# A prefetch hint on all five engines for the branch around a kernel's rarely used general path

## The chip, the cores and the metric

The kernel runs on one core of a Trainium2 chip. The metric is the device time of one execution in microseconds, the median of several runs. Five engines work side by side, each with an instruction stream of its own: TensorE (PE in the profile, with its weight loads as PEld), VectorE (DVE), ScalarE (ACT), GpSimd (POOL) and SyncE (SP), which here only issues transfers.

## The reference

One block of a network over x of shape (8, 512, 256), in float32: a layer norm, windowed causal attention with 16 heads of 16 and rotary positions, and a three-layer network with weights of plus and minus one, whose output passes through silu and gates the attention.

```
xn = _layernorm(x, axis=-1)
# attention: q, k rotated; window of 250 keys, causal
mask = (delta >= 0) & (delta < CONTEXT)
scores = where(mask, einsum('bhtd,bhsd->bhts', q, k) * D ** -0.5, min)
s = (softmax(scores) @ v) @ out_proj_w.T
# network: w = where(k, 1, -1)
h = s0 * (concatenate([xn, -xn]) @ w(k0));  h = relu(h) * 2
h = s1 * (h @ w(k1));                       h = relu(h) * 2
g = _silu(s2 * (h @ w(k2)))
x = x + s * g
```

## The kernel before

The work is done sequence by sequence (`b` from 0 to 7), with tokens in tiles of 128 and features in chunks of 128. Two kinds of work are interleaved on TensorE: the network's layers (`layer`, L518: per output chunk eight 16-bit matmuls for the high part and eight 32-bit ones for the low part) and the attention's scores and values (L733, L807). ScalarE makes the high parts and exponentials, VectorE the low parts and divisions, GpSimd the masks and some products.

The order is written out by hand. Every piece of work is an entry (time, cost, function) in the list `everything`; `run` sorts it by time, calls each function, and pushes follow-ups that fall due some time later on a planned clock. Inside `tc.manual_schedule` the engines' instructions stand in the order in which these functions issue them. Times are in a planned unit in which one sequence takes `SEQ` = 42; the last sequence (b = 7) begins at 294. The numbers only order the pieces: 338.06 is the last output chunk of the second layer, 339.78 and 341.65 the third layer's last two parts, 341.6 `add_up`, and 343.52 to 346.22 the output projections (`project_o`, L916).

The kernel takes a fast path that is exact only while some quantities stay within limits. While it runs, the tiles that meet the limits are counted in `counts`. `add_up` sums these counts (L975 to L978) to one integer, `whole`. After the schedule every engine loads that integer into a register (L1025), and compares it with the number of rows: if any row failed, everything is computed again in a general, slow way.

```
    n_rows = P * 2 * B * T + B * T
    found = nc.values_load(whole[0:1, 0:1], min_val=0, max_val=n_rows)
...
    with tc.If(found < n_rows):
        for b in range(B):
```

The body of the `If` (L1072 to L1088, with `shifted` from L1027) is some thousands of instructions on each of TensorE, GpSimd, ScalarE and VectorE, and it stands in each stream between the branch and the end of the program. On the other side of the branch stand a few semaphore instructions, and then the end of the program: SP waits for all transfers and engines, and a barrier of all five follows (L1144).

The last pieces of the fast path on each engine, which the prediction follows, are: the sigmoid of the gate at L584 to L590, its earlier form at L624 to L635, the output products at L928 to L945, and the stores to `out_dram` at L932 and L946. The residual is loaded at L552.

Of the kernel before, what the change touches and what calls it, by code (L numbers as in the profile page):

```python
# [34 lines left out]
def tile_attention_times_gated_ffn(  # L35
# [44 lines left out]
    B, T, E = x.shape  # L80
# [30 lines left out]
    def load_x(b, t):  # L111
        xs[b, t] = xpool.tile([P, E], F32, tag=f"x{t}", name=f"x_{b}_{t}")
        queue = nc.scalar if b == 0 and t >= NT // 2 else nc.sync
        queue.dma_start(xs[b, t], x[b, ts(t, P), :])
# [98 lines left out]
    SEQ = 42.0  # L213
# [12 lines left out]
    def run(pieces):  # L226
        clock, count_, due = 0.0, itertools.count(), []

        def follow(at, more):
            for delay, f in more if isinstance(more, list) else ():  # L230
                heapq.heappush(due, (at + delay, next(count_), f))

        for _, cost, f in sorted(pieces, key=lambda piece: piece[0]):
            while due and due[0][0] <= clock:
                at, _, g = heapq.heappop(due)
                follow(at, g())
            more = f()
            clock += cost
            follow(clock, more)
        while due:  # L240
            at, _, g = heapq.heappop(due)
            follow(at, g())
# [109 lines left out]
    def first_parts(*tiles):  # L352
        for t in tiles:
            for f in states[0].pop(("parts", t)):
                f()
# [96 lines left out]
    def stack(b, g):  # L452
        st = states[b]
        for what in ("k0", "q0", "q1"):
            t = stacks.tile([P, T], F32R, tag=what, name=f"{what}_{b}_{g}")
            rows = st["dram", what[0], int(what[1])][32 * g : 32 * g + 32]
            nc.sync.dma_start(t.bitcast(F32), rows.rearrange("p n t -> (p n) t"))
            st[what, g] = t

    def prepare(b, plain=False):  # L460

        if b == 0 or plain:
            at = dict(stats=-40, norm=-38, x=-36, k=0, q=3, v=9.2)
            dp, dv = 1.5, 1.5
        else:

            at = dict(load=9, stats=9, down=10.5, over=12, norm=16.8, k=21.8, q=24.8, v=SEQ + 0.6)
            if b == 1:
                at.update(load=18.65, stats=15, down=18, over=18.7, norm=24.8, k=26.6, q=28.4)
            dp, dv = 1.5, 1.0  # L470
            at = {n: SEQ * (b - 1) + f for n, f in at.items()}
        out = [(at["stats"], 0, lambda: stats(b))]
        if "over" in at:
            out += [
                (at["load"], 0, lambda: load_xT(b)), (at["down"], 0, lambda: lay_down(b)),
                (at["over"], 0, lambda: lay_over(b)),
                (at["norm"], 0, lambda: norm_turned(b, 0)),
                (at["norm"] + 1.2, 0, lambda: norm_turned(b, 1)),
            ]
        for t in range(NT):  # L480
            if "over" not in at:
                out += [
                    (at["norm"] + t, 0, lambda t=t: norm(b, t)),
                    (at["x"] + t, 0.25, lambda t=t: turn_x(b, t, plain)),
                ]
            out.append((at["v"] + dv * t, 0.87, lambda t=t: project_v(b, t)))
        for what in "kq":
            for n, part in enumerate("ab"):
                if b == 0 and what == "k" and not plain:

                    out += [
                        (-34.3 if n == 0 else -32.95, 0.87, lambda p=part: project(b, "k", p, 0)),
                        (at["k"] + dp * n, 0.87, lambda p=part: project(b, "k", p, 1)),
                    ]
                else:
                    out.append((
                        at[what] + dp * n, 1.75, lambda w=what, p=part: project(b, w, p),
                    ))
        return out
# [32 lines left out]
    def outputs(b):  # L532

        n = 1 if b + 1 < B else 2
        return [(f, ts(half, T // n)) for half in range(n) for f in range(EC)]
# [67 lines left out]
    def plain_ffn(b):  # L603

        st = states[b]
        for name, src, w in (("h1p", "xp", w0["l"]), ("h2p", "h1p", w1["l"])):
            h = st[name] = hpool.tile(
                [P, NF0, T], F32, tag=name[:2] + "l", name=f"{name}_{b}"
            )
            n = w.shape[1]  # L610
            for f in range(NF0):
                ps = ps_m.tile([P, T], F32, tag="mm", name=f"f_h_{b}_{f}")
                for c in range(n):
                    nc.tensor.matmul(
                        ps, w[:, c, ts(f, P)].bitcast(F32), st[src][:, c, :],
                        start=(c == 0), stop=(c == n - 1),
                    )
                nc.scalar.activation(h[:, f], ps, AF.Relu)
# [36 lines left out]
    def finish_ffn(b, u, how):  # L655
        quick.add(last_at(b, u))
        out = [(last_at(b, u), L3 * (2 if b + 1 < B else 1), lambda: last(b, u, how))]
        if how == "later":
            out.append((late(b, u) - 4.5, 0, lambda: gate_ready(b, u)))
        return out  # L660
# [157 lines left out]
    def keep(b, g, po):  # L818

        st = states[b]  # L820
        if g % 2 == 0:
            for name, rows in (("V", first_half), ("S", second_half)):
                tile_ = st["half", name] = outs.tile(
                    [P, T], F32, tag=f"{name}{g // 2}", name=f"{name}_{b}_{g}",
                    bufs=2 if name == "V" else 1,
                )
                nc.scalar.mul(tile_, po, rows)
        else:
            for name, rows in (("V", second_half), ("S", first_half)):
                tile_ = st[name, g // 2] = st.pop(("half", name))  # L830
                nc.vector.scalar_tensor_tensor(tile_, po, rows, tile_, ALU.mult, ALU.add)
# [118 lines left out]
    def finish(b, final=False):  # L950
        out = []
        for u in range(len(outputs(b))):
            out.append((
                late(b, u), 1.75 if b + 1 < B else 0.87,
                lambda u=u: project_o(b, u, final),
            ))
        return out

    def divisions(b):
        out = []  # L960
        for pair in range(2):
            if b + 1 < B:
                first, d = (SEQ * b + 30.0, 2.0) if pair == 0 else (SEQ * (b + 1) + 4.2, 2.0)
            else:
                first, d = SEQ * b + (22.5 if pair == 0 else 33.6), 1.3
            for n in range(4):
                out.append((first + d * n, 0, lambda p=pair, n=n: invert(b, p, n)))
            out.append((first + d * 4, 0, lambda p=pair: divide(b, p)))
        return out
# [3 lines left out]
    def add_up():  # L973
# [3 lines left out]
        nc.vector.tensor_reduce(found_f, total, mybir.AxisListType.X, ALU.add)  # L977
        nc.vector.tensor_copy(whole, found_f)  # L978

    outs = None  # L980

    def swap():
# [6 lines left out]
        (-31.0, 0, lambda: enough(0)),  # L989
        (-32.7, 0, lambda: first_parts(2, 3)),  # L990
        (19.2, 0, make_w2), (22.5, 0, swap), (SEQ * (B - 1) + 47.6, 0, add_up),
    ]
    for c in range(EC):
        everything += [
# [29 lines left out]
    n_rows = P * 2 * B * T + B * T  # L1024
    found = nc.values_load(whole[0:1, 0:1], min_val=0, max_val=n_rows)  # L1025
# [43 lines left out]
                stop=(j == n // P - 1),  # L1069
            )  # L1070

    with tc.If(found < n_rows):  # L1072
        for b in range(B):
            for t in range(NT):
                load_x(b, t)
            run(prepare(b, plain=True))
            plain_ffn(b)
            for u in range(len(outputs(b))):
                run(finish_ffn(b, u, "at once"))
            for g in range(NG):  # L1080
                stack(b, g)
                po = ps_o.tile([P, T], F32, tag="po", name=f"f_po_{b}_{g}")
                for t in range(NT):
                    for r in range(4):
                        shifted(b, g, t, r, po)
                keep(b, g, po)
            run(divisions(b))
            run(finish(b))  # L1088
# [59 lines left out]
```

## Time and profile before

| | us |
|---|---|
| median of three runs | 607.96 (607.72 to 608.24) |
| profiled execution: first to last instruction (span) | 607.0 |
| what the median has around the span | 0.9 |
| TensorE busy | 594.8 (98%) |
| VectorE, ScalarE, GpSimd busy | 383.5, 294.7, 309.0 |
| last matmul ends | 598.9 |
| last compute (VectorE, L945) ends | 600.7 |

The span counts from the first to the last recorded instruction, the sequencers' own (branches, semaphores, drains) among them, while "busy" counts compute alone. In the lists, an engine's name with a q (SPq) is its sequencer. L1072 is line 1072 of the kernel.

### The profile page before, as it was taken

What the parts mean: (1) busy time and instruction counts of PE and PEld (TensorE: products, weight loads), DVE (VectorE), ACT (ScalarE), POOL (GpSimd) and SP (SyncE); (2) the same over time, 40 slices, a digit from 0 to 9 for tenths busy, and PEclk for the clock granted to TensorE, in tenths of its full rate; (3) what the DMA queues carried; (4) which work ended last, traced back from release to release, by engine and by line L of the source; (5) the groups of instructions that cost most, each with busy time, mean ns of one, the idle gap of its engine ahead of it and who ended that gap; (6) DMA issues with size and microseconds to landing.
All of it is one profiled execution on the core that took longest, in us unless ns stands there. A gap on an engine that the chain in (4) does not pass through costs nothing. (4 is left out here: it accounts for less than half of the span.)

```text
span 607.0 us, 11176 instructions
## 1 busy us (share of the span) xinstructions
PE 594.8 (98%) x4492; PEld 367.2 (60%) x4492; DVE 383.5 (63%) x606; ACT 294.7 (49%) x414; POOL 309.0 (51%) x368
## 2 busy tenths in 40 slices
PE   7999999999999999999999999999999999999994
PEld 6654666555655556556565566555666555657783
DVE  6864637558467485665856657666666557554774
ACT  4676664354554535445453454542554445555321
POOL 2975542466533663445724557235662456627632
PEclk9999999999999999999999999999999999999998
DMA  8552722226331443315243252421642216222201
GB/s 273 216 187 94 272 87 88 86 106 207 105 122 53 176 138 105 122 65 216 85 134 108 106 210 78 142 94 70 210 131 94 88 69 243 71 65 77 71 1 41
DMA packets 38061, 74.51 MB, mean 123 GB/s; under 512 B 5360, under 2 KB 13040, under 8 KB 38000
## 3 DMA queue, kind: packets, MB, share of 16 engines
q1 hardware_dynamic: 35568, 71.48, 34.0%
q10 hardware_dynamic: 2432, 2.23, 1.2%
q8 instruction: 37, 0.61, 0.4%
q14 instruction: 24, 0.20, 0.1%
HBM read 44.30 MB, written 29.39 MB: 121 GB/s over the span
## 5 line engine op out<-in xcount | busy, mean ns | idle before, releaser
L752 ACT ACTIVATE p<-sc 128x1024 f32<-128x1024 f32 (+2 forms) x144 | 138.3, 1012 | 74.9 <-PE sc L733 45.1
L768 POOL TENSOR_SCALAR_AFFINE_SELECT p<-p 128x512 f32<-128x512 f32 x128 | 91.3, 719 | 127.4 <-ACT p L752 127.4
L518 PE MATMUL h_ps<-h1l,w1l_sb 128*128 128x512 f32 (+1 forms) x576 | 146.2, 396 | 0.0
L518 PE MATMUL h_ps<-h1h,w1h_sb 128*128 128x512 f16 (+1 forms) x576 | 123.1, 356 | 0.0
L518 PEld LDWEIGHTS h_ps<-h1l,w1l_sb 128*128 128x128 f32 x576 | 100.2, 188 | 29.5 <-issue 9.2
L529 ACT ACTIVATE h2h<-h_ps 128x512 f16<-128x512 f32 (+1 forms) x72 | 39.4, 548 | 112.6 <-PE h_ps L518 112.6
L518 PEld LDWEIGHTS <-w1h_sb 128*128 128x128 f16 x576 | 51.2, 98 | 58.8 <-issue 17.5
L775 POOL TENSOR_SCALAR_AFFINE_SELECT p<-p 128x512 f32<-128x512 f32 (+1 forms) x96 | 49.3, 513 | 71.4 <-ACT p L752 71.4
L807 PE MATMUL po<-p,v_pad 128*32 128x378 f32 (+4 forms) x1216 | 76.5, 372 | 0.0
L633 DVE RECIPROCAL den<-den 128x256 f32<-128x256 f32 (+1 forms) x32 | 52.5, 1644 | 24.9 <-POOL den L628 24.9
L733 PEld LDWEIGHTS sc<-q,k 32*128 32x128 f32 x1216 | 44.2, 184 | 30.4 <-issue 21.1
L527 DVE SCALAR_TENSOR_TENSOR h2l<-h_ps,h2h 128x512 fp32r<-128x512 f32 (+1 forms) x72 | 43.8, 609 | 29.6 <-ACT h2h L529 29.6
L527 DVE SCALAR_TENSOR_TENSOR h1l<-h_ps,h1h 128x512 fp32r<-128x512 f32 x64 | 42.7, 680 | 25.7 <-ACT h1h L529 25.6
L733 PE MATMUL sc<-q,k 32*128 32x378 f32 (+4 forms) x1216 | 58.1, 306 | 0.6 <-DMA q<-dq 0.3
L884 DVE RECIPROCAL S<-S 128x128 f32<-128x128 f32 x64 | 57.5, 920 | 0.1
L518 PE MATMUL h_ps<-xl,w0l_sb 128*128 128x512 f32 x128 | 52.3, 489 | 0.0
L807 PEld LDWEIGHTS po<-p,v_pad 128*32 128x32 f32 x1216 | 31.7, 109 | 28.4 <-issue 17.0
L529 ACT ACTIVATE h1h<-h_ps 128x512 f16<-128x512 f32 x64 | 38.0, 598 | 18.7 <-PE h_ps L518 18.6
L301 DVE TENSOR_TENSOR xT<-xT,of_all 128x512 f32<-128x512 f32 x28 | 22.3, 801 | 28.4 <-DMA of_all<-d 27.9
L518 PE MATMUL h_ps<-xh,w0h_sb 128*128 128x512 f16 x128 | 38.4, 382 | 0.1
L572 PE MATMUL z_ps<-h2l,w2l_sb 128*128 128x512 f32 (+1 forms) x144 | 36.1, 391 | 0.2 <-DVE h2l L527 0.2
L425 POOL TENSOR_TENSOR m_ka<-m_ka,m_kb 128x512 f32<-128x512 f32 x16 | 20.1, 1276 | 28.5 <-DVE m_kb L404 28.5
(101 smaller groups left out, 735.1 us busy)
## 6 DMA issues: line engine op xcount, KB each, us to landing
q<-dq SPq DMA_DIRECT2D x64, 256.0 KB, 3.5
dq<-qh SPq DMA_DIRECT2D x16, 512.0 KB, 3.1
dq<-m_qa SPq DMA_DIRECT2D x16, 512.0 KB, 5.5
k<-dk SPq DMA_DIRECT2D x32, 256.0 KB, 2.7
dk<-kh SPq DMA_DIRECT2D x8, 512.0 KB, 2.9
dk<-m_ka SPq DMA_DIRECT2D x8, 512.0 KB, 2.9
x<-in_x_dram SPq DMA_DIRECT2D x30, 128.0 KB, 2.7
xT<-in_x_t_dram SPq DMA_DIRECT2D x7, 512.0 KB, 5.6
```

What stands on the lines that cost most here:

```text
L301: nc.vector.tensor_tensor(xT, xT, st["of_all"][:, i], op)
L518: nc.tensor.matmul(ph, w[p][:, c, ts(f, P)], st[src + p][:, c, cols], start=(k == 0), stop=(k == n - 1),)
L527: nc.vector.scalar_tensor_tensor(lo, ph, 0.0, hi, ALU.max, ALU.subtract)
L529: high = lambda: nc.scalar.activation(hi, ph, AF.Relu)
L572: nc.tensor.matmul(pz, w2[p][:, c, ts(f, P)], st["h2" + p][:, c, cols], start=(c == 0 and p == "h"), stop=(c == NF1 - 1 and p == "l"),)
L633: nc.vector.reciprocal(part, part)
L733: nc.tensor.matmul(sc[r // 2][:, r % 2, ds(off, n)], st["k0", g][row, ts(j, P)], st[f"q{turn}", g][row, ds(j * P + first, n)], start=(turn ...
L752: nc.scalar.activation(p[:, 2 * half : 2 * half + 2, :n], sc[half][:, :, :n], AF.Exp, scale=D ** -0.5,)
L768: nc.gpsimd.affine_select(out=block, in_=block, compare_op=ALU.is_ge, fill=0.0, base=0, pattern=[[0, 4], [1, P]], channel_multiplier=-1,)
L775: nc.gpsimd.affine_select(out=block, in_=block, compare_op=ALU.is_ge, fill=0.0, base=-1, pattern=[[0, 4], [-1, beyond]], channel_multiplier=1,
L807: nc.tensor.matmul(po[32 * r : 32 * r + 32, ds(j * P + first, n)], v_columns(j, g, r), p_[:, r, ds(off, n)], start=(j == 0), stop=(done an ...
L884: nc.vector.reciprocal(part, part)
```

## The change

One entry is added to `everything` at 338.0, which marks a place in the stream of every engine for a hint on the branch called "general"; and the `If` is given that name. Where the hint stands, each engine gets one more instruction. Nothing else in the streams is added, removed or reordered.

```diff
+    def hint():
+        tc.mark_branch_hint_location(
+            "general", "LikelyTaken", engines=list(mybir.ALL_ENGINES)
+        )
+
...
         (19.2, 0, make_w2), (22.5, 0, swap), (SEQ * (B - 1) + 47.6, 0, add_up),
+        (SEQ * (B - 1) + 44.0, 0, hint),
     ]
...
-    with tc.If(found < n_rows):
+    with tc.If(found < n_rows, label="general"):
```

## Prediction

> **What bounds the kernel now.** I read the page from the top: span, busy times, instruction queues.
>
> ```profile
> span 607.0 us, 11176 instructions
> ...
> PE 594.8 (98%) x4492; PEld 367.2 (60%) x4492; DVE 383.5 (63%) x606; ACT 294.7 (49%) x414; POOL 309.0 (51%) x368
> ...
> q8 instruction: 37, 0.61, 0.4%
> q14 instruction: 24, 0.20, 0.1%
> ```
>
> TensorE is busy for 594.8 of 607.0 us, so nearly the whole kernel is its matmuls, and the change touches none of them. What can move is the 12.2 us in which it isn't busy, most of it at the end. The two instruction queues fetch the program itself: 0.61 MB in 37 packets is 16 KB a packet, 0.20 MB in 24 is 8 KB. By the count of packets the first is TensorE's and the second the four smaller engines'.
>
> Next, the view of busy times in stretches, cut at the end of the last compute and at the end of the long gap (columns: length, then busy time and count of each engine, clock, DMA share, GB/s).
>
> ```profile
> 600.00:601.20 1.20, 0.00 (x0) 0.00 (x0) 0.71 (x2) 0.00 (x0) 0.47 (x1) 1.00 0.34 112
> 601.20:605.00 3.80, 0.00 (x0) 0.00 (x0) 0.00 (x0) 0.00 (x0) 0.00 (x0) 0.54 0.27 85
> 605.00:607.04 2.04, 0.00 (x0) 0.00 (x0) 0.00 (x0) 0.00 (x0) 0.00 (x0) 0.50 0.04 12
> ```
>
> The last compute (VectorE, L945) ends at 600.7. Then no engine does anything for over 6 us. The view of line 1072, the branch, says what the sequencers do there (engine, operation, count, ns min/median/max, first and last start).
>
> ```profile
> L1072 SPq EVENT_SEMAPHORE  x8: 17/17/17, 605.1 to 605.7; - x8
> L1072 PEldq COMPARE_BRANCH  x1: 4322/4322/4322, 598.0 to 598.0; - x1
> L1072 POOLq COMPARE_BRANCH  x1: 45/45/45, 600.1 to 600.1; - x1
> L1072 DVEq COMPARE_BRANCH  x1: 76/76/76, 601.0 to 601.0; - x1
> L1072 SPq COMPARE_BRANCH  x1: 45/45/45, 601.2 to 601.2; - x1
> L1072 ACTq COMPARE_BRANCH  x1: 54/54/54, 601.7 to 601.7; - x1
> L1072 PEldq EVENT_SEMAPHORE  x1: 51/51/51, 602.4 to 602.4; - x1
> L1072 POOLq EVENT_SEMAPHORE  x1: 17/17/17, 602.9 to 602.9; - x1
> L1072 DVEq EVENT_SEMAPHORE  x1: 21/21/21, 605.6 to 605.6; - x1
> L1072 ACTq EVENT_SEMAPHORE  x1: 17/17/17, 605.7 to 605.7; - x1
> ```
>
> From branch to next instruction: PE 4.4 us, POOL 2.8, DVE 4.6, SP 3.9, ACT 4.0. No instruction of lines 1027 to 1088 (the general path) is recorded, so every engine jumped over it, and what follows the jump is what arrives late. The waits of SP's queue put SP's gap down to nothing but itself:
>
> ```profile
> SPq L1072 <- SPq L1072: 3.8, 1, 3.8
> ```
>
> Four 8 KB packets of q14 and one of q8's lie between 601 and 604 in the DMA view cut to that stretch: fetches for these jumps. The chain that sets the end is then: last store issued (600.8), SP's branch (601.2), fetch, SP's eight semaphore instructions (from 605.1), SP's final waits and the barrier of all five (607.0). The profiled span is 607.0; the median of the runs, 607.96, has 0.9 us more around it, which I keep.
>
> [...]
>
> **The change part by part.** It adds one hint instruction to each engine's stream, and moves, if it works, five fetches from behind the branch to ahead of it.
>
> *The five hints.* The trace has no such row. Below: nothing, since the sequencers wait for their engines most of the time. [...] I take 0.05 (like the branch records) and put it at zero on the path, since something covers it on every engine. The entry sorts at 338, just before TensorE's last group of L518 matmuls (started at 589.0), behind POOL's L628 (589.1), the rectifier L529 (589.2) and VectorE's L633 (590.5); POOL then idles 2.3 us, ACT 1.4, DVE 0.4. On SP it stands before the last residual loads (L552, the last at 570.8), after which SP waits 26.2 us for the count. TensorE's sequencer runs ahead of the array: its branch executes at 598.0 while matmuls run to 598.9. [...]
>
> *The five fetches.* The same bytes, earlier. DMA is nearly idle from 583 to 590 (one packet). At zero; with no cover, a packet of 8 KB takes 0.3 to 0.5 us of one of 16 engines. From hint to branch there are 9 us or more on each engine (589 to 598 on PE, 590.5 to 601.0 on DVE, 30 on SP), twice the longest gap of 4.6.
>
> *The gap.* If SP's target is there, SP goes on at about 601.4 instead of 605.1, and likewise ACT at 601.9 and DVE at 601.2. This is up to 3.7 us. But what is late next is the stores. SP's eight instructions are one for each DMA semaphore, and they can't pass before the last store has landed:
>
> ```profile
> L946 SPq DMA_DIRECT2D out_dram<-gate x15: 337/338/347, 146.2 to 598.2; - x15
> L932 SPq DMA_DIRECT2D out_dram<-gate x2: 338/518/697, 599.9 to 600.5; - x2
> L946 ACTq DMA_DIRECT2D out_dram<-gate x1: 373/373/373, 600.8 to 600.8; - x1
> ...
> DMA to landing us min/median/max: 2.0/2.0/3.9
> ```
>
> The last stores are issued at 600.5 and 600.8. With the median landing of 2.0 us the last is in at 602.8; with the longest, 3.9 (the store of 598.2, whose landing at 602.1 fell among the fetches), at 604.7. I take 603.7, halfway: the big fetches are out of the way, but each engine, once across, will fetch a further block beside these stores, as it does now after each jump.
>
> After the landing SP needs the rest of its waits and the barrier. Now that is 607.0 − 605.1 = 1.9 us from the first of the eight; the eight take 0.6, and five of them can be done before the landing, so 1.3 to 1.7 are left; I take 1.6. The end comes at 603.7 + 1.6 = 605.3, a gain of 607.0 − 605.3 = 1.7 us. Ends: 602.8 + 1.3 = 604.1 (gain 2.9) and 604.7 + 1.7 = 606.4 (gain 0.6). The time is 607.96 − 1.7 = **606.2**, between 605.0 and 607.3.
>
> **The rivals.**
>
> *The hint does nothing (608.0).* A hint can only help if it still steers a fetch when it executes deep inside the block in which the branch lies. This is the weak place. In the stretch 563 to 601 the DMA view lists three packets on q8 and none on q14:
>
> ```profile
> q1 hardware_dynamic: 931, 0.99, 7.6%
> q8 instruction: 3, 0.05, 0.5%
> ```
>
> So the four smaller engines had their next blocks before 563, long before a hint at 589 (on SP, before 571), and TensorE fetched its last at 585.6, before 589. If the sequencer decides what to fetch only on entering a block, all five hints come too late. [...] Against: the hint has room of 9 us and a free DMA, and nothing else would be its use. Time: 607.96 + 0 to 0.1.
>
> *Only some engines profit, or the stores land late (607.0 to 607.9).* SP's final waits need all five engines across the branch. ACT branches last, at 601.7; if it alone still fetched in the shortest gap seen, 2.8 us (POOL), it would be across at 604.5, and the end at about 605.9; with its own 4.0, at 605.7 and the end where it is. PE and POOL branch early, are across at 602.4 and 602.9 now, and decide nothing.
>
> *The hint's block takes the place of one still needed (slower).* [...] If the target displaces the next block in sequence and an engine steps into that block between hint and branch, it fetches on the spot, 2.8 to 4.6 us. On VectorE that would fall on the chain L589, L590, L931, L938, L945, which issues the last store: 605.3 + 3.7 = 609.0 on the span, so about 609.9. It decides as soon as a block boundary lies among VectorE's last instructions[...]. Against it: q14 is empty from 563 to 601, so no engine crossed a boundary with a fetch there[...]. [...]
>
> **How the numbers follow.** A measurement of this kernel can tell about 0.2%, 1.2 us, from no change. The hint works on the engines that matter: 0.69, of which 0.61 gain over 1.2 us and 0.08 less (late landings, one engine left behind). It does nothing: 0.22. It displaces a needed block: 0.09. So faster 0.61, same 0.30, slower 0.09. The likeliest case gives 606.2, alone 605.0 to 607.3. To leave out no more than 2 in 10 the range must take in "nothing" with its own 0.2 us: 605.0 to 608.2; left out are the slower case and a sliver of gains above 2.9.
>
> **What would show it.** Right: a hint record on each engine near the times above; instruction packets on q8 and q14 near 570 and 588 to 592; at L1072 the next instruction within 0.3 us of the branch on SP, ACT and DVE, and a self-wait of SP there well under 3.8 us; SP's first group held by the landing of the last stores. Wrong: the same gaps of 3 to 5 us at L1072, and q14 again silent until 601 (the hint does nothing), or a new gap of about 4 us on DVE between 590 and 601 (displacement). A change in the TensorE rows before 595 would be none of this.

## The result, and the profile after

| | before | after |
|---|---|---|
| median of 21 runs each, taken side by side | 607.85 us | 606.90 us |
| ratio, after to before | | 0.9982 (0.9976 to 0.9987) |
| profiled execution: span | 607.0 us | 605.0 us |
| last compute (VectorE, L945) ends | 600.75 us | 601.15 us |
| from there to the end of the span, the **tail** | 6.29 us | 3.87 us |

By the ratio, which is taken over all runs, the change gains 0.18%, 1.1 us (0.8 to 1.5); the two medians are 0.95 us apart. The tail alone is 2.4 us shorter. So two things are to be explained: how the tail shrank, and where the other microsecond went.

The parts of the page after that answer to the first fence of the prediction:

```profile
span 605.0 us, 11181 instructions
...
PE 595.0 (98%) x4492; PEld 367.4 (61%) x4492; DVE 382.6 (63%) x606; ACT 294.6 (49%) x414; POOL 310.6 (51%) x368
...
q8 instruction: 36, 0.59, 0.4%
q14 instruction: 20, 0.16, 0.1%
```

Five instructions more, no compute more, and the busy times agree within 1.6 us. But the instruction queues carry less: q14 four packets fewer (24 to 20), q8 one fewer (37 to 36). By the numbers that is one packet for each of the five engines.

The stretches of busy time after, cut like those of before (length, busy time and count of PE, PEld, DVE, ACT, POOL, clock, DMA share, GB/s):

```profile
600.00:601.20 1.20, 0.00 (x0) 0.00 (x0) 1.12 (x3) 0.00 (x0) 0.84 (x1) 1.00 0.05 12
601.20:605.02 3.82, 0.00 (x0) 0.00 (x0) 0.00 (x0) 0.00 (x0) 0.00 (x0) 0.52 0.34 110
```

Compute ends in the first stretch, 0.4 us later than before. The empty time behind it, two stretches of 3.80 and 2.04 before, is now a single one of 3.82. Its DMA share is higher (0.34 against 0.27), since more of the stores' traffic falls into it: the stretch ahead of it has 0.05, where before it had 0.34.

The view of the branch after (line 1078 now, L1072 before; engine, operation, count, ns, first and last start):

```profile
L1078 SPq EVENT_SEMAPHORE  x8: 17/17/17, 601.8 to 603.6; - x8
L1078 PEldq COMPARE_BRANCH  x1: 393/393/393, 598.4 to 598.4; - x1
L1078 PEldq EVENT_SEMAPHORE  x1: 51/51/51, 599.4 to 599.4; - x1
...
L1078 SPq COMPARE_BRANCH  x1: 70/70/70, 601.3 to 601.3; - x1
L1078 DVEq COMPARE_BRANCH  x1: 89/89/89, 601.4 to 601.4; - x1
L1078 DVEq EVENT_SEMAPHORE  x1: 21/21/21, 602.0 to 602.0; - x1
...
```

From the branch to the next instruction it is now 0.5 us on SP, 0.6 on VectorE, 0.5 on ScalarE, 0.9 on TensorE, where it was 3.9, 4.7, 4.0 and 4.4. (GpSimd: 0.5 for 2.7.) The hint works on all five. The first row says what is late next: SP's eight instructions, packed into 0.6 us before, now stretch over 1.8. Seen one by one, five of them follow the branch at once (601.81 to 602.15), the sixth comes at 603.07 and the last two at 603.58 and 603.65. The stores explain the two late steps. The view of line 932 has SP's:

```profile
L932 SPq DMA_DIRECT2D out_dram<-gate x2: 333/336/338, 600.3 to 600.9; - x2
...
DMA to landing us min/median/max: 1.8/1.8/1.8
```

The view gives the landing of the first of the two alone. By the semaphore updates in the trace the second, issued at 600.9, lands at 603.05 and ScalarE's, the last, at 603.56; SP's sixth and seventh instruction, which wait for these two, start 0.02 us after each. In the waits of SP's queue this is still booked on SP itself, in three pieces of at most 0.9 us instead of one of 3.8:

```profile
SPq L1078 <- SPq L1078: 1.9, 3, 0.9
```

The same updates show something in the kernel before that its views don't: there SP's second store, issued at 600.5, landed only at 605.15, 4.7 us later, and in a second trace of that kernel at 605.28. Of the stores' own packets one alone moved after 603, while five fetches did (DMA view of before, cut to 603 to 607.04):

```profile
q14 instruction: 4, 0.03, 2.7%
q8 instruction: 1, 0.02, 1.5%
q1 hardware_dynamic: 1, 0.00, 0.0%
```

So two things were late at 605.1, SP's instructions behind the branch (the first at 605.1) and this store. Had all the gaps gone and this store still landed at 605.15, SP's sixth instruction would have come at about 605.17 instead of 605.53, and the tail would be some 0.4 us shorter (an estimate from these two numbers), not 2.4. With the change both come earlier. What in the fetches could hold a landing back, with the store's last packet gone at 603.0, isn't shown.

Last, the view of line 1150, the end of the schedule, where the hints are booked:

```profile
L1150 POOLq BRANCH_PREFETCH_HINT  x1: 43/43/43, 0.7 to 0.7; - x1
...
L1150 SPq BRANCH_PREFETCH_HINT  x1: 51/51/51, 0.8 to 0.8; - x1
...
```

The other three are like these, TensorE's the last: all stand at the very front of the streams, at 0.7 to 0.9 us, and not at 570 to 590. The entry at 338.0 in the plan doesn't set their place. The branches whose gaps are short now come some 600 us later, at 598.4 to 602.2 us.

The two profiles can't be compared by their spans. In the profiled executions that list both, the time is the span + 1.7 us (605.02 gives 606.75, 607.13 gives 608.86). The profiled execution of before was thus itself about 608.8 long, 0.9 above its median. The traces of before and after differ in the first 90 us only: from there on, TensorE's matmuls after stand 0.41 us behind those of before, constant to about 0.01 us, until the tail. How late the first 90 us end varies from execution to execution: two traces of one kernel, here taken three times, end them up to 0.6 us apart, and three of the kernels below were caught in executions that were 2.5 to 3.3 us behind before there. The tail can nearly be read from one trace (it repeats within 0.05 us after, and within 0.44 before). The front has to be read from medians.

### The profile page after: what moved, and what is told of

The parts are those of the page before. It is cut to its first block, busy times and chain, and to the rows that moved or that the text cites. A ratio compares the mean times of both kernels' runs of the same rounds, so it can differ in the third digit from the quotient of the medians.

```text
span 605.0 us, 11181 instructions
## 1 busy us (share of the span) xinstructions
PE 595.0 (98%) x4492; PEld 367.4 (61%) x4492; DVE 382.6 (63%) x606; ACT 294.6 (49%) x414; POOL 310.6 (51%) x368
## 5 line engine op out<-in xcount | busy, mean ns | idle before, releaser
L775 POOL TENSOR_SCALAR_AFFINE_SELECT p<-p 128x512 f32<-128x512 f32 (+1 forms) x96 | 49.3, 514 | 72.6 <-ACT p L752 69.2
L807 PE MATMUL po<-p,v_pad 128*32 128x378 f32 (+4 forms) x1216 | 76.7, 372 | 0.1
L807 PEld LDWEIGHTS po<-p,v_pad 128*32 128x32 f32 x1216 | 31.8, 109 | 28.7 <-issue 17.0
```

The costliest lines, as they stand in the source:

```text
L775: nc.gpsimd.affine_select(out=block, in_=block, compare_op=ALU.is_ge, fill=0.0, base=-1, pattern=[[0, 4], [-1, beyond]], channel_multiplier=1,
L807: nc.tensor.matmul(po[32 * r : 32 * r + 32, ds(j * P + first, n)], v_columns(j, g, r), p_[:, r, ds(off, n)], start=(j == 0), stop=(done an ...
```

## Experiments

All are timed beside the kernel before on the same chip; "time" is the ratio to it and its interval. Tail is the length defined above. "Lost" is the tail's gain (against 6.07, the mean of the two traces of before, 6.29 and 5.85) less the gain in time (the ratio times 608 us): what a kernel gives away ahead of the tail. It is good to about half a microsecond, and less so in the plain near-target kernel, which has six runs.

| kernel | hints | time | gain, us | tail, us | lost, us |
|---|---|---|---|---|---|
| before, again | none | 1.0001 (0.9990 to 1.0012) | −0.1 | 5.85 | |
| after (the result) | five, front | 0.9982 (0.9976 to 0.9987) | 1.1 | 3.87 | 1.1 |
| after, again | five, front | 0.9985 (0.9977 to 0.9993) | 0.9 | 3.84 | 1.3 |
| after, a third time | five, front | 0.9978 (0.9969 to 0.9987) | 1.3 | 3.89 | 0.8 |
| near target, plain | none | 0.9955 (0.9940 to 0.9971) | 2.7 | 3.33 | 0.0 |
| near target, hints | five, front | 0.9980 (0.9971 to 0.9989) | 1.2 | 3.30 | 1.6 |
| late | five, where planned | 0.9991 (0.9983 to 0.9998) | 0.5 | 5.50 | 0.0 |
| middle | five, inside | 0.9970 (0.9959 to 0.9981) | 1.8 | 4.16 | 0.1 |
| SP and ScalarE in front | two front, three inside | 0.9975 (0.9966 to 0.9985) | 1.5 | 3.84 | 0.7 |
| the others in front | three front, two inside | 0.9977 (0.9969 to 0.9984) | 1.4 | 3.93 | 0.7 |
| three | three, inside | 0.9972 (0.9964 to 0.9980) | 1.7 | 3.58 | 0.8 |
| three, again | three, inside | 0.9966 (0.9953 to 0.9979) | 2.1 | 3.66 | 0.3 |
| one memset more | five, inside | 0.9992 (0.9978 to 1.0006) | 0.5 | 4.20 | 1.4 |

### Both kernels again

The edit is none: the changed kernel twice more, and the kernel before once more under the same treatment.

> The changed kernel once more, for a second profile and for comparison with the others on this chip. Its profile had lost 2.4 us after the last compute (6.3 to 3.9) and was 0.4 later before it, 2.0 in all, while the timed runs lost 1.0. Theory A (the profiled execution of the kernel before overstates the gap at the branch; timed runs have a smaller one): span about 605.0 again, time about 1.0 under the kernel before. Theory B (the gap is as long in timed runs, and the hints give back over 1 us elsewhere, in the start or in the fetches): the 0.4 us ahead of the last compute is there again, and the time is again 1.0 under.

> The kernel before once more, for a second profile: its first was an execution with a tail of 6.3 us after the last compute. From the kernel with the general path left out (time 2.7 under, tail 3.3) a typical tail of 5.9 to 6.0 follows. Gaps at the branch of 2.7 to 4.7 us again; ratio 1.000 within 0.1%.

> The changed kernel on the same chip and in the same rounds as the one before. 0.9 to 1.1 under the kernel before; tail 3.9, L775 late by 0.3 again, front later by about 1 us in all.

The kernel before gives 1.0001 of itself. The changed one gives 0.9985 and 0.9978; all three intervals of it lie under 1 and overlap. So the gain is there, and about 1.1 us (for the third, 1.3 is over the 0.9 to 1.1 expected). The three tails of after agree within 0.05 us; the two of before differ by 0.44. VectorE's and SP's gaps are 4.3 and 3.4 us in the repeat, for 4.7 and 3.9: the gap varies from trace to trace, so against the repeat the tail's gain is 2.0, not 2.4. Either is well above the time gained, as theory B has it.

### A target close by, with and without hints

The body of the `If` is emptied in each stream, so that the branch jumps over a few instructions. The general path is left out of these two kernels; it isn't executed on this data. One has no hints, the other the five of the change.

```diff
+def no_general_path(nc):
+    for f in nc.m.functions:
+        for b in f.blocks:
+            if b.name.endswith("_true"):
+                b.instructions = [i for i in b.instructions
+                    if type(i).__name__ == "InstUnconditionalBranch"]
```

> No hints; the general path is left out of the program (of its block only a branch stays), so that the target of the branch is the next instruction and nothing has to be fetched out of sequence. The floor without any hint. Theory A: about 1.0 to 1.3 us under the kernel before, near the changed kernel. Theory B: 2.3 to 2.8 under the kernel before, so over 1 us better than the changed kernel. Both: in the profile the gap at the branch is under 0.5 us on each engine and the tail after the last compute about 3.6 to 3.9.

> The same as the one before without the general path, but with the five hints: what the hints alone cost, where they can gain nothing. Theory A: 0 to 0.15 us above the kernel without hints (0.1 at the start of SP's and ScalarE's first transfers). Theory B: some 1.3 us above it.

Without hints the branch of the plain kernel, in the view of line 1072:

```profile
L1072 SPq EVENT_SEMAPHORE  x8: 17/17/17, 603.6 to 605.1; - x8
...
L1072 SPq COMPARE_BRANCH  x1: 45/45/45, 603.4 to 603.4; - x1
```

SP is across in 0.2 us, the others in 0.2 to 0.3 (TensorE 0.9), and SP then waits for the stores as in the changed kernel. So the gap of before (2.7 to 4.7 us) is the price of the distance, and not of the branch, but for the 0.2 to 0.3 us that are left here, on TensorE 0.9 of 4.4 (for it the expected 0.5 was missed). This profiled execution ran late from its start (PE waited 1.8 us for the transfer of `wqkv_sb`, and its time was 608.3 where the median is 605.7), which is why 603.4 stands where after has 601.3.

This kernel also shows what the fetches do to the stores. Its DMA view from 598 to the end lists no instruction packet, and by the semaphore updates its four last stores all land 1.7 to 1.8 us after their issue, and so do those of its pair with hints. After, with five packets in that stretch, they take 1.8 to 3.2 us, and before, with ten up to the end, 2.5 to 4.7. So in these traces the last stores land later where fetches run beside them, and what the hints leave of this is most of the 0.5 us by which the tail of after (3.87) exceeds the plain one's (3.33): its last store takes 2.4 us, for 1.8 here.

The pair shows the price of the hints, because here they can gain nothing: the tails are 3.33 and 3.30. The plain kernel gains 2.7 us (1.8 to 3.6), just what its tail gives. The one with hints gains 1.2 (0.7 to 1.8). Five hints at the front cost about **1.5 us**, at five records of some 50 ns. The intervals of the two ratios only touch, so there is a cost, but with only six runs of the plain kernel its size is rough.

### The hints where the plan puts them

Each hint is moved to the place that the prediction assumed: ahead of the instruction that is last but n of its engine.

```diff
+    last_but = {"PE": 82, "DVE": 14, "Activation": 9, "Pool": 6, "SP": 10}
+    for engine, n in last_but.items():
+        own = [i for i in block.instructions if i.engine.name == engine]
+        hint, place = own[0], own[-1 - n].name
+        rest = [i for i in block.instructions if i.name != hint.name]
+        at = [i.name for i in rest].index(place)
+        block.instructions = rest[:at] + [hint] + rest[at:]
```

> The changed kernel with each hint moved from the start of its stream to the place that the plan's 338.0 stands for: before the last L518 group on PE, behind L633 on DVE, L529 on ACT, L628 on POOL, L552 on SP[...]. Theory E (what to fetch is decided when a block is entered): the gaps at the branch are back (2.8 to 4.6 us) on all five and the time is that of the kernel before, within 0.2. Theory H (a hint steers a fetch whenever it executes, 7 us or more ahead): gaps under 1 us, time that of the changed kernel or 0.1 under it.

The hints' records, in the view of line 1166 (the same place as L1150 above), and then the branch:

```profile
L1166 SPq BRANCH_PREFETCH_HINT  x1: 50/50/50, 570.4 to 570.4; - x1
L1166 PEldq BRANCH_PREFETCH_HINT  x1: 45/45/45, 587.1 to 587.1; - x1
...
L1166 DVEq BRANCH_PREFETCH_HINT  x1: 56/56/56, 590.6 to 590.6; - x1
```

```profile
L1078 SPq EVENT_SEMAPHORE  x8: 17/17/17, 604.4 to 605.0; - x8
L1078 PEldq COMPARE_BRANCH  x1: 393/393/393, 598.1 to 598.1; - x1
L1078 PEldq EVENT_SEMAPHORE  x1: 51/51/51, 599.1 to 599.1; - x1
...
L1078 SPq COMPARE_BRANCH  x1: 70/70/70, 601.3 to 601.3; - x1
...
```

The hints execute 10 to 31 us ahead of their branches. On SP, VectorE, ScalarE and GpSimd they do nothing: the gaps are 3.1, 3.65, 3.0 and 2.7 us, the whole page counts 24 packets on q14, as before, and SP's eight instructions are again packed behind a long gap. On TensorE the hint works. Its gap is 0.9 us, and the DMA view cut to 586.5 to 598 shows the fetch, where the kernel before has no packet at all:

```profile
q8 instruction: 1, 0.02, 0.5%
```

That packet, of 16 KB, moves at 589.2, two microseconds after the hint. So on TensorE the late hint started a fetch here, and on the four others, by their gaps and the 24 packets, none. Why the engines differ isn't shown; what the trace of before does show is that q14 carries no packet from 563 to 601, so that there the last fetch of the four smaller engines ahead of their branches lies before the times of all their hints here (570.4 to 590.6). Neither theory thus holds for all five. The gaps of SP, VectorE and ScalarE are shorter than in the first trace of before by 0.7 to 1.1 us, and than in its repeat by 0.2 to 0.7; TensorE's 16 KB moved at 589.2 here and at 599.89 before; whether that is what shortened them wasn't isolated. The gain of 0.5 us and the tail of 5.50 fit each other.

### The hints inside the streams

The same mover with `own[n]`, counted from the front, puts the hints behind the busy start and long before the branch. Five inside; then two halves, in which the engines named keep their hint at the front. The three lists stand below one another here; each kernel has one.

```diff
-    last_but = {"PE": 82, "DVE": 14, "Activation": 9, "Pool": 6, "SP": 10}
+    # middle:
+    first = {"PE": 1500, "DVE": 190, "Activation": 140, "Pool": 120, "SP": 90}
+    # SP and ScalarE stay in front:
+    first = {"PE": 1500, "DVE": 190, "Pool": 120}
+    # TensorE, VectorE and GpSimd stay in front:
+    first = {"Activation": 140, "SP": 90}
```

> All five hints, moved from the start of each stream to a place well inside it (behind 89 instructions on SP, 119 on POOL, 139 on ACT, 189 on DVE, 1499 on PE), so that they delay nothing in the first microseconds and still execute before the block of the branch is entered. If hints at the start cost some 1.5 us by shifting the first transfers, and a hint has to come before its block: tail after the last compute 3.8 to 3.9 as in the changed kernel, time 2.2 to 2.5 us under the kernel before (ratio about 0.996), about 1.3 under the changed kernel. If the cost comes from being armed, wherever: as the changed kernel, 1.0 under.

> SP's and ACT's hints stay at the start of their streams (ahead of all first loads), the other three are moved inside. If the cost of the start comes from the loads of the input issued 0.1 us later and in another order: tail 3.9 and time about 1.0 to 1.3 under the kernel before. If it comes from PE, DVE and POOL: about 2.3 under.

> The reverse: PE's, DVE's and POOL's hints stay at the start, SP's and ACT's are moved inside. If the loads are the cause: about 1.9 to 2.2 under the kernel before, 0.3 to 0.4 of the cost being left at L775 on POOL, which was late by that in all three kernels with a hint ahead of it and in neither of those without. If the other three engines are the cause: 1.0 under.

With five inside, at 176 to 211 us, the hints work as well as at the front (gap on SP and ScalarE 0.5, on TensorE 0.9), for branches at 598 to 602 us: to be first in its stream wasn't needed. The time is 0.9970, 1.8 us under before instead of the 2.2 to 2.5 expected; the tail of this trace, 4.16, is 0.3 longer than expected, and with it 0.1 is lost ahead of the tail. Its interval (0.9959 to 0.9981) overlaps with the change's, so that it beats the change is likely but not shown by the times. The halves give 0.9975 and 0.9977, between the two, and neither of their expected pairs of numbers is met. Which engine's hint costs how much isn't settled by the times.

The traces do isolate one part. TensorE's loads of L807 at 70 us, after, then before (an engine's wait is listed by what ended it: us, times):

```profile
L807 PEld LDWEIGHTS po<-p,v_pad x16: 106/108/110, 70.0 to 70.7; 128*32 128x32 f32 x16
...
  POOL p L768: 0.4, 1
  POOL p L775: 0.3, 1
```

```profile
L807 PEld LDWEIGHTS po<-p,v_pad x16: 106/108/109, 69.8 to 70.3; 128*32 128x32 f32 x16
...
  POOL p L768: 0.3, 1
```

A second wait of 0.3 us, for GpSimd's mask of L775, is there after and not before. The loads end 0.4 us later, and nothing downstream makes up for it: this step stays to the end of the trace. It is in every trace in which one instruction more stands ahead of L775 on GpSimd from the front (after three times, near target with hints, and the half with GpSimd in front), where TensorE falls back by 0.4 us from 65 to 75 us against before, and in none of the eight others (one memset more aside, which comes next).

### One instruction more on GpSimd, and no hint in force

To tell whether it is the hint or its place in the stream, the middle version gets one small memset among GpSimd's first instructions. At 70 us no engine has met a hint yet.

```diff
     nc.gpsimd.memset(v_pad, 1.0)
+    one_more = const.tile([P, 1], F32, name="one_more")
+    nc.gpsimd.memset(one_more, 1.0)
```

> The hints inside the streams, as in the kernel with all five moved inside, and one more instruction (a memset of 128x1) among the first on POOL, where the hint stood: every later POOL instruction moves one place up in its stream. If L775 at 69 us is late by 0.3 because of that place (the instruction then stands first in a block that has to be entered): late again here, and L807 on PE with it. If it is late because a hint is armed on POOL: on time, since the hint comes only at 190 us.

The step at L807 (L809 in this kernel) is back, 0.4 us, without a hint in force. So it is one instruction more in the stream and not the hint: a plain memset does the same. Why one place in the stream costs TensorE these 0.4 us isn't shown; that L775 then stands first in a block was the author's guess. The ratio is 0.9992 (0.9978 to 1.0006), 1.3 us above the middle version's, though the two intervals overlap; more than the step is in it. In this trace TensorE also falls back by another 0.4 us between 100 and 590 us, which happens in no other; what causes it wasn't isolated.

### Three hints are enough

TensorE and GpSimd branch early. Without their hints, and with the other three inside:

```diff
-            "general", "LikelyTaken", engines=list(mybir.ALL_ENGINES)
+            "general", "LikelyTaken",
+            engines=[mybir.EngineType.SP, mybir.EngineType.DVE, mybir.EngineType.Activation]
...
+    first = {"DVE": 190, "Activation": 140, "SP": 90}
```

> Hints on SP, ACT and DVE alone, inside the streams. PE and POOL jump early and are across by 602.9 even without, so if only the late engines matter the time is that of all five, 2.2 to 2.5 under the kernel before. If the fetches of PE and POOL (at 599.9 and 601.2) hold up the landing of the last stores, on which SP waits next: tail 4.3 to 5, time 1.2 to 2.0 under.

> The three hints on SP, ACT and DVE inside the streams, once more, beside the changed kernel on the same chip: the best version so far. Tail 3.6 to 3.9, front (time to the end of the last compute) that of the kernel before; 1.6 to 2.0 under the kernel before and 0.5 to 0.9 under the changed kernel.

From the repeat, the view of the branch:

```profile
L1078 PEldq COMPARE_BRANCH  x1: 3438/3438/3438, 598.0 to 598.0; - x1
...
L1078 PEldq EVENT_SEMAPHORE  x1: 51/51/51, 601.5 to 601.5; - x1
```

TensorE waits for 3.4 us at its branch again (4.3 before the change) and is across at 601.5; GpSimd at 602.9. The last store lands at 602.9 as well, so they hold up nothing, and the tail is 3.6 to 3.7 us, no longer than with five, where 4.3 to 5 were expected if these two fetches slowed the stores. The two runs, 0.9972 and 0.9966, are with the middle version (0.9970) the best of the kernels that keep the general path, and clearly under before. Against the change itself, in the same rounds, it is 0.9966 to 0.9978: 0.1% better by the point, with overlapping intervals, so not shown.

## Why the prediction was right, and where not

Forecast 606.2, measured 606.9, inside the range; the likeliest case (hints work, then the stores are late) is what happened. But three of its steps were wrong. Two of these cancel, by luck; the third had no effect only because the hints stood elsewhere than assumed.

**The place of the hints: wrong.** They aren't at 338 in the plan but first in each stream. In the place that the prediction worked with, the change would have gained 0.5 us, as the late version shows. Of the rivals, "the hint does nothing" named the true weak point, a hint that comes too late: in the late version, 10 to 31 us ahead of the branch, the gaps stay at 2.7 to 3.65 us on four of five engines. It was given 0.22, and with the place that was assumed it deserved more than half.

**The fetches: right in sign, not in place.** In the kernel after, one fetch per engine has disappeared by the counts (20 packets for 24 on q14, 36 for 37 on q8), q14 is empty from 563 to 601.4 as it was before, and 4 packets of it instead of 8 follow the jumps. When the target came, and in place of what, isn't shown; no trace shows what a packet holds. The prediction's picture (five fetches moved from behind the branch to 570 to 592) was of the right sign; what it expected to see near 570 and 590 isn't there. The jump itself cost 2.7 to 4.7 us in the trace of before (the prediction's 2.8 and 4.6 are differences of rounded starts), and 0.2 to 0.3 with the target near (TensorE 0.9). Two details of the trace of before were misread: five packets of q14, not four, lie between 601 and 604, and the q8 packet there moves at 603.17, after TensorE is across at 602.4; the one between TensorE's branch (598.0) and its next instruction moved at 599.89. The next instruction was also expected within 0.3 us of a hinted branch, and came after 0.5 to 0.6.

**The hints at zero: wrong by about 1 us.** The term was put at zero, from branch records of some 50 ns and cover on every engine. The records are 43 to 51 ns, but at the front there is no cover: the first loads go out at 0.87 and 0.89 us instead of 0.79. The near pair measures the price as about 1.5 us, the account of the three runs of after as 0.8 to 1.3. Shown of it are 0.1 at the start and 0.4 at L807; some 0.6 is left open. That another short instruction at the front of the other four engines would cost as much wasn't tried. The prediction's test "a change in TensorE's rows before 595 would be none of this" pointed away from this cost.

**The gap and the stores: right, too cautious.** SP was held by the landing of the last stores as predicted. The landing was put at 603.7, 3.0 us after the end of compute; it was 603.56 against 601.15, or 2.4. The range for it came from the landings that the view lists, 2.0 to 3.9 us; the store that landed last before had taken 4.7, which that view leaves out. After, SP's two take 1.8 and 2.2 us to land (2.5 and 4.7 before), so the further fetches beside them still cost something, against the 1.7 to 1.8 of the near target, but less than was feared; that q14 has 4 packets there for 8 goes with it, but wasn't isolated as the cause. The rest of the waits and the barrier took 1.46 for 1.6. The tail came to 3.87 where the steps give 605.3 − 600.7 = 4.6. This undersized the gain by 0.7, which hides most of the microsecond lost in front.

**"0.9 us around the span": wrong in its parts.** It is 1.7 around, in an execution that was 0.8 over the median that the prediction had (607.96). This has no effect on the difference, as the sum was made against that execution.

**The other rivals.** "Only some engines profit" did not occur; its side remark that TensorE and GpSimd decide nothing is shown by the version with three hints. "Displaces a block still needed" did not occur: VectorE has no gap of 4 us between 590 and 601 (its longest wait there is 2.4 us, as before). The gain of 0.18% (0.13 to 0.24) falls on the 0.2% that the prediction took as the least it could tell.

## What to carry to other kernels

Look behind the last compute: several microseconds in which nothing is busy and SP waits for itself after a branch (3.8 us here) went with a hint, or with a target close by, down to the next limit, the landing of the last stores. Place the hint behind the crowded start and well ahead of the branch (at 176 to 211 us it worked here on all five engines for branches at 598 to 602, 10 to 31 us ahead of them on TensorE alone), and look in the trace where it ended up; hints on the engines that branch last were enough here. Five instructions of 50 ns cost about a microsecond at the front of this tightly ordered kernel, so measure a change of this kind by medians and read the trace stretch by stretch.

## What the runs showed of the hardware

- The jump over the general path cost 2.5 to 4.7 us from branch to next instruction without a hint, the jump over a few instructions 0.2 to 0.3 (TensorE 0.9), and the hinted far one 0.5 to 0.6 (TensorE 0.9).
- A hint given at 0.7 to 0.9 us still worked at the branches at 598 to 602 (gaps of 0.5 to 0.9 us). With it there are fewer fetches, not more: 20 packets for 24 on q14, 36 for 37 on q8.
- A hint 10 to 31 us before the branch left SP, VectorE, ScalarE and GpSimd their gaps (2.7 to 3.65 us); on TensorE, 11 us before, it worked (gap 0.9), with the fetch 2 us after the hint.
- One more small instruction at the front of GpSimd's stream, a hint or a memset, delayed TensorE at 70 us by 0.4 us.
- A last store of 128 KB landed 1.7 to 1.8 us after its issue with no fetch beside it, after 1.8 to 3.2 with the fetches that five hints left, and after 2.5 to 4.7 with those behind five unhinted jumps.
- Two traces of one kernel ended their first 90 us up to 0.6 us apart, and stayed parallel within 0.03 us from there to the tail.
